# Four graph layers on one core: stored edge matrices loaded sooner into buffers of their own, and edges numbered by ScalarE and TensorE from a transposed adjacency

## The chip, the cores and the metric

The kernel runs on one core of a Trainium2 chip. The metric is the device time of one execution in microseconds, from the first instruction to the last.

## The reference

Eight batches of 2048 nodes with 128 features pass through four layers over one sparse symmetric adjacency (each pair is joined with a chance of about 1/128, and every node with itself). Layers 0 and 2 are multi-head attention with a feed-forward part; layers 1 and 3 are graph attention with additive scores.

```python
def mha(adj, h):                     # layers 0 and 2, 8 heads of 16
    Q, K, V = h @ Wq, h @ Wk, h @ Wv             # split into heads
    scores = einsum('bnhd,bmhd->bhnm', Q, K) / sqrt(16)
    scores = where(adj == 0, -inf, scores)
    x = layer_norm(h + softmax(scores) @ V @ Wo + bo)
    return layer_norm(x + relu(x @ W1 + b1) @ W2 + b2)

def gat(adj, x):                     # layers 1 and 3
    h = x @ W
    e = leaky_relu((h @ a_src)[:, :, None] + (h @ a_dst)[:, None, :], 0.2)
    e = where(adj == 0, -inf, e)
    return layer_norm(softmax(e) @ h + x)

x = gat(adj, mha(adj, gat(adj, mha(adj, x))))
```

## The kernel before

The kernel does not compute dense attention. It turns the adjacency into lists of edges and gathers only the rows of neighbours. (A dense version, `Dense`, stands behind a branch that is taken only where the lists overflow; it is not run here.)

**Units and tiles.** The nodes are cut into 32 units of 64 nodes. A unit holds its edges in nine tiles of 128 slots, handled as `TG` = 5 steps t = 0 to 4, two tiles a step and one in the last. For each unit there is a matrix `hot` (128 x 960): its first 640 columns send a query to the slots of its edges, its last 320 sum slots back to their owners. Layers 1 and 3 rebuild `hot` from a few numbers; layers 0 and 2 load it from DRAM, where it was stored in 8 bits (`self.hots`).

**Lists.** `block_list(adj, i)` works on 128 nodes, so there are 16 blocks, two units each. It loads 128 rows of the integer adjacency (1 MB) into a `kv` buffer, and one VectorE instruction (L1134) turns them into numbers: 0 where there is no edge, and otherwise 2048 minus the column, from the constant `falling`; its accumulator gives `seen[0]`, the sum of the numbers. Sixteen `max` instructions (L1152) take the eight largest of each 128 columns into `cand`, and five rounds of `max` and `match_replace` (L1171, L1173) take the 40 largest of those. L1174 counts them, L1177 sums them into `seen[1]`. `unit_list` then builds each unit's `hot` (ScalarE L1297, L1299, L1301; TensorE L1321; VectorE L1347, L1350, L1390), its gather indices (L1369), and an 8-bit copy `hot8` (ScalarE L1376) that is stored to DRAM (L1380), by POOL's queue for the first 12 units and by SP's afterwards. The 8-bit copies of units 0 to 2 are kept in their buffers until layer 0 uses them.

**Layer 0 and 2 (`attention`).** `opened` calls `fetch` for a unit: a load of x (L1444), a load of the stored matrix into a `hot8` buffer (L1459), and its conversion into a `hot` buffer by ScalarE (L1466). Each step then gathers keys and values (POOL, L1764), spreads queries over slots (TensorE, L1825), multiplies (VectorE, L1837), reduces to scores (VectorE, L1844), takes exponentials (ScalarE, L1854), weighs the values (POOL, L1870; in some steps VectorE), and sums into the unit's accumulator (TensorE, L1922). After step 4, `after_attention` normalizes (it begins with L1981 on VectorE), runs the output product, both norms and the feed-forward part, writes x to DRAM (L1432) and projects it for the next layer (L1626 or L1628, copies L1544 and L1546, stores L1683 or L1686).

**What sets the order.** Every operation is recorded with a cost, a key and the buffers that it takes; `Plan.order` plays them through before anything is issued, giving each engine the ready operation with the lowest key whose buffers are free. The result is a fixed sequence for each engine. An operation that `holds` a cell takes that buffer when it is issued itself. The list of block i has key `10 * i - LEAD` with `LEAD` = 60, and unit u's steps have keys from `5 * u`, so a list is built about 12 units ahead of its use. In `BY_KEY` stand the tags whose buffers are given out strictly in order of keys. An operation with `port=True` does not start while the other of VectorE and POOL runs one. `hot` has three buffers, shared by lists and attention, `hot8` five, `kv` six, and the PSUM tag `m` three banks, used by nearly all small products.

The head, before the first gather, projects all of x into the key and value table (`load`, `project`) and builds the first lists.

Of the kernel before, what the change touches and what calls it, by code (L numbers as in the profile page):

```python
# [48 lines left out]
ADJ = (-1499, -1495, -1487, -1479, -1471)  # L49

SBUF_BUFS = {
    "kv": 6, "hot": 3, "hot8": 5, "x": 4, "q_sb": 2, "rows": 3, "at": 1, "r": 2, "x1": 2, "hidden": 1, "normed": 2,
    "xnew": 2, "trows": 2, "s": 2, "ex": 7, "var": 2, "rstd": 2, "rc": 2, "te": 2, "e": 4, "w": 3,
    "cand": 2, "aux": 3, "aux16": 3, "unit_aux": 2, "some": 2, "rank_e": 2, "pick": 1,
    "gap": 1, "late": 1,
}
BY_KEY = ("kv", "hot", "x", "q_sb", "acc")
PSUM_BUFS = {"q": 1, "acc": 1, "m": 3}

NEG = -57344.0  # L60
# [742 lines left out]
class Sparse:  # L803
# [12 lines left out]

    def __init__(self, ctx, tc, x, xt, xk, adj, w, out):
        self.tc, self.nc, self.w, self.xt_in, self.xk_in, self.out = tc, tc.nc, w, xt, xk, out  # L820
        self.B, self.N, _ = x.shape
        self.NB = self.N // P
        self.NU = self.N // UNIT
        self.HB = self.B // 2

        def pool(name, **kw):
            return ctx.enter_context(tc.tile_pool(name=name, **kw))

        self.nc.scalar.preload_act_table_set("natural_log_exp_and_others")
        self.const = pool("const", bufs=1)  # L830
        self.dram = pool("dram", bufs=1, space=DRAM)
        self.plan = Plan(self.nc)
        self.op, self.cell = self.plan.op, self.plan.cell
        for tag, bufs in SBUF_BUFS.items():
            self.plan.pool(tag, pool(f"sb_{tag}", bufs=bufs), bufs, tag in BY_KEY)
        for tag, bufs in PSUM_BUFS.items():
            self.plan.pool(tag, pool(f"ps_{tag}", bufs=bufs, space=PSUM), bufs)

        self.constants()
        self.weights_at = [Cell() for _ in LAYERS]  # L840
        self.keys_at = Cell()
        self.late = self.tight = False
        self.whole()
        self.gates = {}

        self.gate = self.keys_at
        keys = self.const.tile([P, 2 * P], F32, name="Wkv_0")
        self.fill(0, (keys[:, 0:P], w[0]["Wk"]), (keys[:, P : 2 * P], w[0]["Wv"]), at=self.keys_at)
        self.layers = [{"Wkv": keys}]


        self.tables = [
            self.dram.tile([self.N, self.B * (2 * P if kind is MHA else P + 2)], F32, name=f"table_{n}")
            for n, kind in enumerate(LAYERS)
        ]
        self.table = [Cell() for _ in LAYERS]
        self.rest = [Cell() for _ in LAYERS]

        self.xd = self.dram.tile([self.NU, P, CH], F32, name="xd")
        self.x_at = [Cell() for _ in range(self.NU)]  # L860
        self.hots = self.dram.tile([self.NU, P, HOT], F8, name="hots")
        self.hots_at = [Cell() for _ in range(self.NU)]
        self.kept = {}
        self.ends_at = [None] * self.NU
        self.t = self.const.tile([P, self.NU, P // GROUP * self.HB], F32, name="t")
        self.t_at = [Cell() for _ in range(self.NU)]
        self.idx = self.const.tile([P, self.NU, TILES], I32, name="idx")
        self.idx_at = [Cell() for _ in range(self.NU)]


        self.owner = self.const.tile([P, self.NU, TG, 2], F16, name="owner")
        self.ends = self.const.tile([P, self.NU, 2], F32, name="ends")
        self.late_ends = self.const.tile([P, LATE, 2], F32, name="late_ends")
        self.shift = self.const.tile([P, LATE, 2], F16, name="shift")

        self.empty = self.const.tile([P, self.NU, TILES], F32, name="empty")


        self.seen = self.const.tile([P, 4, self.NB], F32, name="seen")
        self.stats = self.const.tile([P, 6], F32, name="stats")  # L880
        self.eps = self.fixed("eps", EPS)
        self.half = self.fixed("half", 0.5)
        self.rows_n = self.fixed("rows_n", float(self.N))
        self.huge = self.fixed("huge", 1e30)
# [3 lines left out]
    def constants(self):  # L888
# [27 lines left out]
        for pattern, base, step, part in (  # L916
# [12 lines left out]
            channel_multiplier=0,  # L929
            allow_small_or_imprecise_dtypes=True,  # L930
        )

        self.centre = const.tile([P, P], F32, name="centre")
        nc.vector.tensor_scalar(self.centre, self.ident, -1.0 / P, None, ALU.add)
# [182 lines left out]
    def block_list(self, adj, i):  # L1117
# [11 lines left out]
        )  # L1129
        if i < len(ADJ):  # L1130
            self.clear(buf, ADJ[i])
        op(
            {"DVE": 2.4},
            lambda e: e.scalar_tensor_tensor(  # L1134
                buf.tile[:, N : 2 * N],
                buf.tile[:, 0:N].bitcast(I32),
                0.0,
                self.falling,
                ALU.not_equal,
                ALU.mult,  # L1140
                accum_out=self.seen[:, 0, i : i + 1],
            ),
            key,
            writes=[buf],
            port=True,
        )

        cand = cell("cand", [P, 16, 8])

        def parts(e, q):  # L1150
            for c in range(4 * q, 4 * q + 4):
                e.max(out=cand.tile[:, c, :], in_=buf.tile[:, N + c * N // 16 : N + (c + 1) * N // 16])  # L1152

        for q in range(4):
            op({"DVE": 0.9}, lambda e, q=q: parts(e, q), key + 0.1, reads=[buf], writes=[cand])


        late = 2 * i < LATE
        wide = WIDE + 3 * late
# [3 lines left out]
        def largest(e):  # L1163
            c = cand.tile.rearrange("p q c -> p (q c)")
            if late:
                e.tensor_scalar(
                    some.tile[:, 0:8], cand.tile[:, 15, :], 0.0, 0.0, ALU.is_gt, ALU.add, accum_out=aux.tile[:, DEG + 1 :]
                )
            for r in range(DEG // 8):
                top = aux.tile[:, 8 * r : 8 * r + 8]  # L1170
                e.max(out=top, in_=c)  # L1171
                if r < DEG // 8 - 1:
                    e.match_replace(out=c, in_to_replace=top, in_values=c, imm_value=0.0)  # L1173
            e.tensor_scalar(  # L1174
                some.tile, aux.tile[:, 0:DEG], 0.0, 0.0, ALU.is_gt, ALU.add, accum_out=aux.tile[:, DEG : DEG + 1]
            )
            e.tensor_reduce(self.seen[:, 1, i : i + 1], aux.tile[:, 0:DEG], axis=mybir.AxisListType.X, op=ALU.add)  # L1177
            if late:
                deg = aux.tile[:, DEG : DEG + 1]
                e.tensor_tensor(deg, deg, aux.tile[:, DEG + 1 :], ALU.subtract)  # L1180
# [218 lines left out]
    def parts(self, u):  # L1399

        for hf in range(2):
            yield slice(hf * UNIT, (hf + 1) * UNIT), slice(u * UNIT, (u + 1) * UNIT), hf
# [36 lines left out]
    def fetch(self, n, u, key):  # L1439
# [13 lines left out]
            self.op({"ACT": 1.05}, lambda e: e.copy(hot.tile, hot8.tile), key - 15, reads=[hot8], writes=[hot])  # L1453
            return x, hot
        if LAYERS[n] is MHA:
            hot8 = self.cell("hot8", [P, HOT], F8)
            self.op(
                {"SP": 0.45},
                lambda e: e.dma_start(out=hot8.tile, in_=self.hots[u]),  # L1459
                key,  # L1460
                reads=[self.hots_at[u]],
                writes=[hot8],
                holds=[hot],
                dma=P * HOT,
            )
            self.op({"ACT": 1.05}, lambda e: e.copy(hot.tile, hot8.tile), key + 4, reads=[hot8], writes=[hot])  # L1466
            return x, hot
# [782 lines left out]
    def failed(self):  # L2250

        nc = self.nc
        over = self.const.tile([P, 3, self.NB], F32, name="over")
        nc.vector.tensor_tensor(over[:, 0], self.seen[:, 0], self.seen[:, 1], ALU.not_equal)
        for k, most in ((2, GS), (3, TILES * P)):
            nc.vector.tensor_scalar(over[:, k - 1], self.seen[:, k], float(most), None, ALU.is_gt)
        some = self.const.tile([P, 1], F32, name="some_over")
        nc.vector.tensor_reduce(some, over.rearrange("p a b -> p (a b)"), axis=mybir.AxisListType.X, op=ALU.max)
        ps = self.plan.pools["m"].tile([P, CH], F32, name="ps_n", tag="m")
        nc.tensor.matmul(ps[0:1, 0:1], lhsT=some, rhs=self.ones[:, 0:1], start=True, stop=True)  # L2260
        count = self.const.tile([1, 1], I32, name="count")
        nc.vector.tensor_copy(count, ps[0:1, 0:1])
        return count


# [11 lines left out]
        before[i.engine] = i  # L2277


def net(tc, x, xt, xk, adj, w, out):  # L2280

    with ExitStack() as ctx:
        s = Sparse(ctx, tc, x, xt, xk, adj, w, out)
        s.run(adj)
        count = s.failed()
        in_order(tc)
        failed = tc.nc.values_load(count, min_val=0, max_val=P, skip_runtime_bounds_check_because="a count of partitions")
    with tc.If(failed > 0):
        with ExitStack() as ctx:
            Dense(ctx, tc, x, adj, w, out).run()  # L2290
# [36 lines left out]
```

## Time and profile before

| | us |
|---|---|
| median of three runs | 2874.8 (2871.36 to 2889.16) |
| the profiled execution | 2883.92 |
| its span in the trace | 2882.1 |
| PE busy | 2240.7 (78%) |
| VectorE busy | 2235.1 (78%) |
| ScalarE busy | 1463.8 (51%) |
| POOL busy | 2125.6 (74%) |

The span runs from the first to the last instruction of the trace; the rest of the execution's own time lies around it. The first gather starts at 122.6 us, unit 0 of layer 0 ends at 157.0 and unit 31 at 1110.6 (its L1981). Layer 1 follows until about 1590, layer 2 ends its last unit at 2443.0, and layer 3 takes the rest. Lists are built from 9.8 us (first L1134) to 813 us (last L1376), so most of layer 0 runs beside them. The rows of a waits view name the waiting instruction, what it waited for, the sum in us, how many times and the longest. The lines of the chain of work that ended last give a start, a length and what ran or travelled. Rows of groups by form give the instruction with its tiles and shapes, how many, then busy us and mean ns of one, then idle time before them.

### The profile page before, as it was taken

To read this page: it belongs to the slowest core of one execution; us is meant where nothing else is said; L and a number is where in the kernel's file an instruction comes from. 1 tells how busy PE (TensorE), PEld (TensorE's weight loads), DVE (VectorE), ACT (ScalarE), POOL (GpSimd) and SP (SyncE) were. 2 spreads that over 40 slices of the span, in tenths; PEclk is the share of its full clock that TensorE was granted. 3 is DMA by queue.
4 is the path that set the end of the run, shared out by engine and by line. 5 is a ranking of instruction groups with operands and counts; after the bars stand their busy time and mean duration, and the time that the engine had idled before them with its cause. 6 is when DMAs were issued, how large, how long until landed. Compare 5 with 4: busy or idle time off the path is not lost.

```text
span 2882.1 us, 61343 instructions
## 1 busy us (share of the span) xinstructions
PE 2240.7 (78%) x22816; PEld 1371.7 (48%) x22816; DVE 2235.1 (78%) x3662; ACT 1463.8 (51%) x4968; POOL 2125.6 (74%) x1465
## 2 busy tenths in 40 slices
PE   6577767787788887788786788888888888677775
PEld 4334333343344444666665344444444444565664
DVE  8799887888788897555554888989889889576665
ACT  6555545555555553555554244545545445354443
POOL 1287776778888886666664788889888887677774
PEclk8888898999999999889998799999999999888777
DMA  7888777888899998999999799999999898999996
GB/s 289 318 338 341 302 304 262 347 317 314 329 362 363 384 369 320 371 411 405 403 408 379 284 365 371 365 380 385 376 355 395 348 386 303 360 404 407 397 402 273
DMA packets 248066, 1022.63 MB, mean 355 GB/s; under 512 B 39184, under 2 KB 52880, under 8 KB 175856
## 3 DMA queue, kind: packets, MB, share of 16 engines
q0 software_dynamic: 166464, 864.44, 76.3%
q1 hardware_dynamic: 81296, 154.18, 14.3%
q8 instruction: 183, 3.00, 0.4%
q14 instruction: 123, 1.01, 0.1%
HBM read 978.23 MB, written 88.08 MB: 370 GB/s over the span
## 4 chain that ended last, share of the span: by engine, by line
DMA 33%; PE 19%; POOL 15%; DVE 15%; issue 13%; ACT 4%; POOLq 0%; SPq 0%; DVEq 0%; ACTq 0%
DMA kv<-table,idx 25%; POOL kv L1870 8%; POOL kv L1764 7%; DVE kv L1837 6%; DMA hot<-hots 6%; PE qe L1825 4%; PE acc L1922 4%; PE ps_y L1582 3%; DVE s L1844 2%; PE ps_f L1598 2%; DMA table<-trows 1%; PE ps_p L1626 1%; DVE w L2088 1%; PE ps_t L1555 1%; DVE kv L1870 1%
## 5 line engine op out<-in xcount | busy, mean ns | idle before, releaser
L1764 POOL DMA_INDIRECT kv<-table,idx x1152 | 1189.0, 1032 | 550.5 <-issue 292.3
L1870 POOL TENSOR_TENSOR kv<-kv,ex 128x2048 f32<-128x2048 f32 x260 | 922.5, 3565 | 85.4 <-ACT ex L1854 81.7
L1837 DVE TENSOR_TENSOR kv<-qe,kv 128x2048 f32<-128x2048 f32 (+1 forms) x320 | 663.1, 2072 | 206.6 <-DMA kv<-table,idx 106.2
L1844 DVE TENSOR_REDUCE s<-kv 128x128 f32<-128x2048 f32 (+1 forms) x320 | 660.6, 2064 | 15.7 <-ACT normed L1733 0.5
L1825 PE MATMUL qe<-q_sb,hot 32*128 32x512 f32 (+1 forms) x2304 | 398.6, 697 | 167.2 <-DVE kv L1837 164.5
L1922 PE MATMUL acc<-kv,hot 128*32 128x512 f32 (+1 forms) x2304 | 357.9, 639 | 78.9 <-POOL kv L1870 73.3
L2104 PE MATMUL acc_q<-kv,w 128*32 128x129 f32 (+1 forms) x4608 | 197.8, 308 | 106.0 <-DVE w L2088 93.4
L2088 DVE TENSOR_TENSOR w<-hot,e 128x512 f32<-128x512 f32 (+1 forms) x384 | 221.6, 598 | 67.6 <-ACT e L2078 54.2
L1825 PEld LDWEIGHTS qe<-q_sb,hot 32*128 32x128 f32 (+1 forms) x2304 | 106.3, 196 | 330.7 <-DVE kv L1837 276.5
L1854 ACT ACTIVATE ex<-s 128x128 f32<-128x128 f32 (+1 forms) x320 | 94.8, 297 | 295.3 <-DVE s L1844 260.5
L2104 PEld LDWEIGHTS acc_q<-kv,w 128*32 128x32 f32 (+1 forms) x4608 | 157.8, 127 | 139.3 <-DVE w L2088 109.1
L2066 DVE TENSOR_TENSOR e<-te,kv 128x16 f32<-128x16 f32 (+1 forms) x320 | 58.2, 182 | 194.5 <-DMA kv<-table,idx 192.2
L1598 PE MATMUL ps_f<-x,W 128*128 128x512 f32 (+1 forms) x264 | 160.0, 698 | 50.2 <-ACT x L1743 30.0
L1922 PEld LDWEIGHTS acc<-kv,hot 128*32 128x32 f32 (+1 forms) x2304 | 54.8, 113 | 247.2 <-POOL kv L1870 136.1
L2104 PE MATMUL acc<-kv,w 128*32 128x129 f32 (+1 forms) x2304 | 115.1, 299 | 66.1 <-DVE w L2088 57.1
L1582 PE MATMUL ps_y<-W,hidden 128*128 128x128 f32 x1024 | 164.9, 284 | 0.9 <-ACT hidden L2012 0.8
L1544 ACT COPY trows<-ps_p 128x258 f32<-128x258 f32 (+1 forms) x236 | 111.0, 473 | 102.5 <-PE ps_p L1628 36.1
L2078 ACT ACTIVATE e<-e 128x16 f32<-128x16 f32 (+1 forms) x320 | 65.0, 212 | 192.7 <-DVE e L2073 186.0
L2012 ACT ACTIVATE hidden<-ps_f,b 128x512 f32<-128x512 f32 (+1 forms) x128 | 86.6, 678 | 127.4 <-PE ps_f L1598 124.0
L1582 PEld LDWEIGHTS ps_y<-W,hidden 128*128 128x128 f32 x1024 | 142.7, 200 | 4.2 <-issue 2.4
L1700 ACT ACTIVATE junk<-ps_y 128x128 f32<-128x128 f32 x248 | 68.5, 276 | 130.9 <-PE ps_y L1582 120.2
L1555 PE MATMUL ps_t<-ident,normed 128*128 128x128 f32 x638 | 116.4, 303 | 23.5 <-DVE normed L1735 12.1
(220 smaller groups left out, 4092.7 us busy)
## 6 DMA issues: line engine op xcount, KB each, us to landing
x<-xd SPq DMA_DIRECT2D x96, 256.0 KB
xd<-xnew SPq DMA_DIRECT2D x93, 256.0 KB
kv<-table,idx POOLq DMA_INDIRECT x1152
table<-trows SPq DMA_DIRECT2D x128, 130.0 KB
kv<-adj_dram SPq DMA_DIRECT2D x16, 1024.0 KB
table<-trows SPq DMA_DIRECT2D x32, 512.0 KB
table<-trows SPq DMA_DIRECT2D x64, 256.0 KB
kv<-xk_dram SPq DMA_DIRECT2D x8, 1024.0 KB
```

Source lines behind the costliest of these rows:

```text
L1544: e.copy(out, in_)
L1555: e.transpose(ps.tile[:, b * P : (b + 1) * P], flat(x.tile)[:, b * P : (b + 1) * P], self.ident)
L1582: e.matmul(ps.tile[:, cols], lhsT=of, rhs=w, start=first and b == 0 and k == 0, stop=last and b == count - 1 and k == len(terms) - 1, skip ...
L1598: lambda e: e.matmul(ps.tile, lhsT=w, rhs=x.tile, start=True, stop=True),
L1764: e.indirect_dma_start(out=rows(kv.tile, j), out_offset=None, in_=self.tables[n][0:nodes], in_offset=bass.IndirectOffsetOnAxis(ap=self.idx ...
L1825: e.matmul(qe.tile[:, j, hf, :], lhsT=hot.tile[rows, t * P : (t + 1) * P], rhs=q.tile[rows, :], start=True, stop=True,)
L1837: e.tensor_tensor(k, qe.tile[:, 0:tiles].rearrange("p j h c -> p (j h) c"), k, ALU.mult)
L1844: e.tensor_reduce(s.tile[:, 0 : tiles * heads].rearrange("p (q c) -> p q c", q=2 * tiles), k, axis=mybir.AxisListType.X, op=ALU.add,)
L1870: e.tensor_tensor(v, v, w.unsqueeze(3).to_broadcast([P, 2 * tiles, heads // 2, HD]), ALU.mult)
L1922: e.matmul(out[rows, :], lhsT=hot.tile[:, col : col + GROUP * (3 - tiles)], rhs=rhs[:, 2 * j + hf, :], start=(t == 0), stop=(t == TG - 1),)
L2088: e.tensor_tensor(w.tile[:, :, j : j + tiles, :].rearrange("p x j c -> p j x c"), oh[:, j : j + tiles].unsqueeze(2).to_broadcast(shape), e ...
L2104: e.matmul(acc(b)[at : at + GROUP * (3 - tiles), :], lhsT=w.tile[:, hf * hb + b, j : j + 3 - tiles, :].rearrange("p j c -> p (j c)"), rhs= ...
```

## The change

The stored matrix of layers 0 and 2 is loaded into a tag of its own, `stored`, with two buffers in key order; its load has a key 12 lower and no longer holds a `hot` buffer, which is now taken by the conversion. `hot8` has four buffers in place of five.

The adjacency for lists comes transposed within each 128 x 128 block (prepared with the other inputs; the plain one stays for `Dense`). ScalarE takes the sign of the integers into 16-bit values, with `seen[0]` now the count of edges. `falling` is multiplied by the identity once, block by block, so that a product of a transposed block of signs with it puts the numbers into PSUM in the old orientation. The products go four at a time into a bank of `m`, and the maxima read them there. `seen[1]` becomes the count that L1174 gave. The end check compares sums of counts.

```diff
 SBUF_BUFS = {
-    "kv": 6, "hot": 3, "hot8": 5, "x": 4, ...
+    "kv": 6, "hot": 3, "hot8": 4, "stored": 2, "x": 4, ...
-BY_KEY = ("kv", "hot", "x", "q_sb", "acc")
+BY_KEY = ("kv", "hot", "stored", "x", "q_sb", "acc")
...
+        for c in range(self.NB):
+            part = self.falling[:, c * P : (c + 1) * P]
+            nc.vector.tensor_tensor(part, part, self.ident, ALU.mult)
...
+        def edges():
+            return buf.tile[:, N : N + N // 2].bitcast(F16)
+
         op(
-            {"DVE": 2.4},
-            lambda e: e.scalar_tensor_tensor(
-                buf.tile[:, N : 2 * N],
-                buf.tile[:, 0:N].bitcast(I32),
-                0.0,
-                self.falling,
-                ALU.not_equal,
-                ALU.mult,
-                accum_out=self.seen[:, 0, i : i + 1],
+            {"ACT": 1.7},
+            lambda e: e.activation(
+                edges(), buf.tile[:, 0:N].bitcast(I32), AF.Sign, accum_out=self.seen[:, 0, i : i + 1]
             ),
             key,
             writes=[buf],
-            port=True,
         )
 
         cand = cell("cand", [P, 16, 8])
-
-        def parts(e, q):
-            for c in range(4 * q, 4 * q + 4):
-                e.max(out=cand.tile[:, c, :], in_=buf.tile[:, N + c * N // 16 : N + (c + 1) * N // 16])
-
         for q in range(4):
-            op({"DVE": 0.9}, lambda e, q=q: parts(e, q), key + 0.1, reads=[buf], writes=[cand])
-
+            ps = cell("m", [P, CH], name="ps_a")
+
+            def numbered(e, q=q, ps=ps):
+                for c in range(4):
+                    cols = slice((4 * q + c) * P, (4 * q + c + 1) * P)
+                    e.matmul(
+                        ps.tile[:, c * P : (c + 1) * P],
+                        lhsT=edges()[:, cols],
+                        rhs=self.falling[:, cols],
+                        start=True,
+                        stop=True,
+                    )
+
+            op({"PE": 0.4}, numbered, key + 0.1, reads=[buf], writes=[ps])
+
+            def parts(e, q=q, ps=ps):
+                for c in range(4):
+                    e.max(out=cand.tile[:, 4 * q + c, :], in_=ps.tile[:, c * P : (c + 1) * P])
+
+            op({"DVE": 0.95}, parts, key + 0.1, reads=[ps], **{"joins" if q else "writes": [cand]})
...
-            e.tensor_reduce(self.seen[:, 1, i : i + 1], aux.tile[:, 0:DEG], axis=mybir.AxisListType.X, op=ALU.add)
+            e.tensor_copy(self.seen[:, 1, i : i + 1], aux.tile[:, DEG : DEG + 1])
...
         if LAYERS[n] is MHA:
-            hot8 = self.cell("hot8", [P, HOT], F8)
+            hot8 = self.cell("stored", [P, HOT], F8)
             self.op(
                 {"SP": 0.45},
                 lambda e: e.dma_start(out=hot8.tile, in_=self.hots[u]),
-                key,
+                key - 12,
                 reads=[self.hots_at[u]],
                 writes=[hot8],
-                holds=[hot],
                 dma=P * HOT,
             )
...
+    adjt = adj.reshape(blocks, P, blocks, P).transpose(0, 3, 2, 1).reshape(n_nodes, n_nodes)
```

More of the change, by code (lines that the diff above doesn't have):

```diff
@@ L51 @@
 SBUF_BUFS = {
-    "kv": 6, "hot": 3, "hot8": 5, "x": 4, "q_sb": 2, "rows": 3, "at": 1, "r": 2, "x1": 2, "hidden": 1, "normed": 2,
+    "kv": 6, "hot": 3, "hot8": 4, "stored": 2, "x": 4, "q_sb": 2, "rows": 3, "at": 1, "r": 2, "x1": 2, "hidden": 1, "normed": 2,
     "xnew": 2, "trows": 2, "s": 2, "ex": 7, "var": 2, "rstd": 2, "rc": 2, "te": 2, "e": 4, "w": 3,
@@ L803, with __init__ @@
 class Sparse:
-    def __init__(self, ctx, tc, x, xt, xk, adj, w, out):
+    def __init__(self, ctx, tc, x, xt, xk, w, out):
         self.tc, self.nc, self.w, self.xt_in, self.xk_in, self.out = tc, tc.nc, w, xt, xk, out
@@ L2252, in failed @@
         nc = self.nc
-        over = self.const.tile([P, 3, self.NB], F32, name="over")
-        nc.vector.tensor_tensor(over[:, 0], self.seen[:, 0], self.seen[:, 1], ALU.not_equal)
+        over = self.const.tile([P, 2, self.NB], F32, name="over")
         for k, most in ((2, GS), (3, TILES * P)):
-            nc.vector.tensor_scalar(over[:, k - 1], self.seen[:, k], float(most), None, ALU.is_gt)
-        some = self.const.tile([P, 1], F32, name="some_over")
-        nc.vector.tensor_reduce(some, over.rearrange("p a b -> p (a b)"), axis=mybir.AxisListType.X, op=ALU.max)
+            nc.vector.tensor_scalar(over[:, k - 2], self.seen[:, k], float(most), None, ALU.is_gt)
+        some = self.const.tile([P, 2], F32, name="some_over")
+        nc.vector.tensor_reduce(some[:, 0:1], over.rearrange("p a b -> p (a b)"), axis=mybir.AxisListType.X, op=ALU.max)
+        nc.vector.tensor_tensor(self.seen[:, 0], self.seen[:, 0], self.seen[:, 1], ALU.subtract)
+        nc.vector.tensor_reduce(some[:, 1:2], self.seen[:, 0], axis=mybir.AxisListType.X, op=ALU.add)
         ps = self.plan.pools["m"].tile([P, CH], F32, name="ps_n", tag="m")
-        nc.tensor.matmul(ps[0:1, 0:1], lhsT=some, rhs=self.ones[:, 0:1], start=True, stop=True)
+        nc.tensor.matmul(ps[0:1, 0:2], lhsT=self.ones[:, 0:1], rhs=some, start=True, stop=True)
+        both = self.const.tile([1, 2], F32, name="both_over")
+        nc.vector.tensor_scalar(both, ps[0:1, 0:2], 0.0, None, ALU.not_equal)
         count = self.const.tile([1, 1], I32, name="count")
-        nc.vector.tensor_copy(count, ps[0:1, 0:1])
+        nc.vector.tensor_tensor(count, both[:, 0:1], both[:, 1:2], ALU.add)
         return count
@@ L2277, in in_order, with net @@
         before[i.engine] = i
-def net(tc, x, xt, xk, adj, w, out):
+def net(tc, x, xt, xk, adj, adjt, w, out):
     with ExitStack() as ctx:
-        s = Sparse(ctx, tc, x, xt, xk, adj, w, out)
-        s.run(adj)
+        s = Sparse(ctx, tc, x, xt, xk, w, out)
+        s.run(adjt)
         count = s.failed()
@@ L2311 @@
     xk = parts.transpose(2, 4, 1, 3, 0).reshape(n_nodes // UNIT, P, b * UNIT)
-    args = [give("x_dram", x), give("xt_dram", xt), give("xk_dram", xk), give("adj_dram", np.roll(np.asarray(inputs["adj"]), (-FIRST, -FIRST), axis=(0, 1)))]
+    adj = np.roll(np.asarray(inputs["adj"]), (-FIRST, -FIRST), axis=(0, 1))
+    blocks = n_nodes // P
+    adjt = adj.reshape(blocks, P, blocks, P).transpose(0, 3, 2, 1).reshape(n_nodes, n_nodes)
+    args = [
+        give("x_dram", x),
+        give("xt_dram", xt),
+        give("xk_dram", xk),
+        give("adj_dram", adj),
+        give("adjt_dram", adjt),
+    ]
     weights = []
```

## The prediction

> **What bounds the kernel now.** Read first: stages by the windows view. Its rows are the list phase (units 1 to 19 of layer 0, while later units' edge lists are still being built), the rest of layer 0, the middle of layer 2, and the head before the first gather.
>
> ```profile
> core 0: us, PE busy (x) PEld busy (x) DVE busy (x) ACT busy (x) POOL busy (x), PEclk, DMA share, GB/s
> 189.90:791.00 601.10, 453.55 (x3404) 233.56 (x3401) 501.88 (x645) 325.25 (x1058) 466.74 (x255) 0.89 0.83 315
> 852.70:1067.00 214.30, 181.56 (x1461) 93.35 (x1458) 189.37 (x134) 111.20 (x366) 187.16 (x105) 0.98 0.94 373
> 1690.00:2380.00 690.00, 584.53 (x4656) 301.78 (x4656) 602.31 (x419) 350.94 (x1168) 589.07 (x330) 0.97 0.94 372
> 0.00:122.00 122.00, 81.03 (x362) 61.84 (x363) 103.42 (x389) 80.20 (x233) 12.25 (x50) 0.89 0.79 294
> ```
>
> VectorE is the busiest engine in the first three rows. In the trace a unit ends with L1981 on VectorE: 189.9 for unit 1, 791.0 for unit 19, so 601.1/18 = 33.4 us a unit with lists. Units 21 to 29 end at 852.7 and 1058.0: 25.7 us each. A list-phase unit costs VectorE 501.9/18 = 27.9 us, yet fills it only to 0.835, against 189.4/214.3 = 0.884 later. So something besides work holds this phase. The waits view for layer 0 (us in total, times, longest), and one row for layer 2, tell what:
>
> ```profile
> PEld qe L1825 <- DVE kv L1837: 137.5, 91, 11.3
> ACT ex L1854 <- DVE s L1844: 114.3, 70, 13.3
> POOL kv L1764 <- issue: 94.3, 203, 11.4
> ACT hot L1466 <- DMA hot<-hots: 89.2, 21, 11.5
> ...
> ACT hot L1466 <- DMA hot<-hots: 21.7, 8, 7.7
> ```
>
> The last two rows are ScalarE standing at the conversion of a stored matrix that has not landed. ScalarE's queue is in order: behind L1466 stand the exponentials L1854, which POOL's L1870 needs, and the norms. In 189.9 to 791.0 this wait is 76.4 us, 4.2 us of each 33.4 us unit. The chain that ended last goes through these loads again and again (start, length, what):
>
> ```profile
> 416.93 15.83 DMA hot<-hots
> ...
> 452.18 13.65 DMA hot<-hots
> ...
> 555.74 16.44 DMA hot<-hots
> ```
>
> The loop behind it: a list unit frees its hot buffer at L1376, the load is issued (416.98 for unit 10), it lands, and ScalarE has stood 11.5 us at L1466 until 432.8.
>
> The rows of the work that is moved off VectorE, and rows that price its replacements:
>
> ```profile
> L1134 DVE SCALAR_TENSOR_TENSOR kv<-kv,falling 128x2048 f32<-128x2048 int32 x16 | 44.8, 2802 | 4.3 <-DMA kv<-adj_dram 4.3
> L1152 DVE MAX8 cand<-kv 128x8 f32<-128x128 f32 x256 | 52.3, 278 | 0.1
> L1702 DVE BATCH_NORM_STATS2 stats<-r 128x6 f32<-128x128 f32 x9 | 2.6, 294 | 0.3
> L1702 DVE BATCH_NORM_STATS2 stats<-ps_y 128x6 f32<-128x128 f32 x8 | 2.4, 294 | 1.0 <-PE ps_y L1582 0.6 <-ACT junk L1700 0.4
> L1544 ACT COPY trows<-ps_p 128x512 f32<-128x512 f32 x111 | 64.9, 589 | 44.2 <-PE ps_p L1626 35.5 <-PE ps_aux L1261 3.5 <-DMA table<-trows 3.2
> L1544 ACT COPY trows<-ps_p 128x258 f32<-128x258 f32 x125 | 46.1, 369 | 58.3 <-PE ps_p L1628 36.1 <-DVE t L1666 21.9
> ```
>
> and one of the timeline of TensorE (start, length, line, count):
>
> ```profile
> 680.55 0.35 PE L1321 MATMUL ps_l<-unit_aux,hot 128*128 128x86 f16 x5
> ```
>
> **The change part by part.** *Loads of stored matrices.* The same 61 loads of 120 KB go out on the same SP queue, but ask for no hot buffer, and rank 12 keys (about two units) earlier. In the built order, the VectorE work standing between such a load's issue and its conversion was 2 to 14 us in the list phase, against transfers of 8 to 16 us; in the changed order it is 31 to 58 us. For the first two units of layer 2 it is over 300 us, for the third 16, then about 40. SP passes its table and xd stores with them and is mostly idle, waiting for results (L1432 on ScalarE's xnew alone 691 us), so moved issues of about 0.5 us cost nothing; without that idle time they would cost 61 x 0.5 = 30 us spread over the run. The hot buffer is also free from issue to landing, which a list can use.
>
> What is the wait worth? Two ways for the list phase. Taken whole, it is 89.2 us. From load: after the change VectorE needs 27.9 - 1.5 = 26.4 us a unit (the 1.5 is next); at the later phase's 0.884 that is a unit of 29.9 us, 3.5 us less over 18 units = 63 us. The second already contains the friction that replaces a wait, so I take 62, with bounds of 22 (a quarter of the wait) and 112 (whole wait and all of VectorE's relief there). Layer 2: 21.7 us, of which 3.5 + 7.7 = 11.2 stand at the junction of layers 1 and 2, where gathers stop too; I take 14, bounds 5 and 22. What is late next is VectorE itself, then POOL (25.9 us of L1764 and L1870 a unit; at its later 0.873 that is 29.7).
>
> *Numbering.* Out of VectorE go L1134 with its accumulator read (44.8 + 1.3) and the reduction L1177 (3.0): 49.1 us; in comes a one-column copy, 16 x 0.16 (the one-column L1233 takes 0.153): net 46.6, or 1.46 a unit. The 256 maxima stay but read PSUM. The statistics rows above take 294 ns from SBUF and 294 from PSUM, so I take no change; the dearest pair is L2150 from PSUM (218 ns, eight columns) against L2073 from SBUF (171): 47 ns more, 12 us over all, 0.4 a unit. [...]
>
> ScalarE gets 16 Sign passes over 2048 columns. The two copies give (589-369)/254 = 0.87 ns a column, so 589 + 1536 x 0.87 = 1.92 us, plus an accumulator read of 0.19: 2.1 us, 34 us in all, 17 of them in the eight blocks of layer 0. It carries 18.1 us a unit of 33.4, so the work lies beside VectorE's; without that room it would cost 1.05 a unit, 17 us. The price for integer input is not shown on ScalarE; VectorE's 2283 ns median for it equals its 2286 for f32 at L1837. Zero and 17 are the bounds; I take the friction already in the 0.884.
>
> Sign also takes over the wait for adjacency, and ScalarE's queue stands behind it. The trace's records of that transfer show 8.4 to 12.6 us from issue to landing in layer 0. The changed order puts 5 to 14 us of VectorE work, 9 to 20 of ScalarE work, between the two, so 0 to 4 us of wait in some of eight blocks: bounds 0 and 32 us, taken 6, inside that friction too.
>
> TensorE gets 256 products of 128 columns; five of 86 columns take 0.35 us together in that row, so four take about 0.4: 26 us in all, 13 in layer 0, beside a load of 25.2 us in 33.4. Each group borrows one of three "m" banks until its maxima are done (a rival below).
>
> *Head.* 16 products over the numbering constant, 0.225 each by L1313, put 3.6 us on VectorE while the first adjacency travels (it lands at 9.5). VectorE loses about 20 us there and ScalarE gains 17 plus two waits: with hot8 cut from 5 to 4 and three kept, units 4 and 5 wait for the store before them (unit 3's goes out at 65.4 and lands at 71.9), about 5 us each. 80 + 17 + 10 = 107 us of ScalarE under a head of 122, while the table's stores move anyway. I take 0, bounds -10 and +10. The end check adds three small operations, about 0.6 us. Layers 1 and 3 hold none of the edited work.
>
> **Sum**: 62 + 14 + 0 - 0.6, so 75 us less. The profiled execution took 2883.9 us (span 2882.1), 9 above the median of 2874.8: 2809 by its clock, 2800 by the median.
>
> **The rivals.**
> *The wait changes its name (2850 us).* ScalarE's stand at the stored matrix turns into a stand at adjacency and at VectorE; only a third of the 110.9 us comes back, 37, and 12 go to Sign (1.5 us for each of eight blocks): 25 net. For it: the leads for adjacency are near its 8.4 to 12.6 us, and L1854 already waits 114 us for VectorE. Against it: the phase's load of 0.835, which more work-bound phases exceed.
> *All of it was on the path (2741 us).* 110.9 of waits and half of VectorE's 46.6 us: 134. For it: 80.3 us for units 8 and 9 held 22 us of this wait; without it they would have taken 29. Against: units 10 to 12 had 1.7 us of it and still took 30.3 each.
> *PSUM banks (2911 us, slower).* The numbered blocks take 64 more turns of the "m" pool, whose three banks also carry each unit's ps_t, ps_o, ps_f, ps_y. In the built order a group stands up to 5 us of VectorE work ahead of its maxima, and TensorE, in order, stops where a unit's next step finds no bank. With 32 groups in layer 0, 75/32 = 2.4 us of delay per group undoes the gain; 3.5 us makes 112 - 75 = 37 us slower. For it: in the head ps_p waits for trows, a bank's reader, 5.0 + 3.9 us. Against: no such row is among the 25 longest of layer 0, with five such turns a block already.
>
> **How the numbers follow.** Forecast 0.62, on its own 2765 to 2835; name change 0.16; all on the path 0.12; banks 0.10. A measurement of this kernel tells about 1% (29 us) from no change: half of the name change falls within it. So faster 0.82, same 0.08, slower 0.10. The range runs from 2740 to 2865, leaving out the banks and thin edges.
>
> **What would show it.** Right: L1466's wait (its new line) under 15 us in all; units 1 to 19 at about 30 us; VectorE's load there near 0.88; Sign near 2.1 us; maxima still near 280 ns; the first gather within 10 us of 122. Wrong: Sign waiting over 30 us for adjacency; PE waiting for maxima; units still above 32 us, which would say that order or POOL, not the load, set their length.

## The result, and the profile after

The changed kernel takes 2839.2 us (median of six runs, 2833.9 to 2846.9) against 2880.9 for the kernel before on the same chip: a ratio of 0.986, 95% interval 0.983 to 0.988. Run again later beside other kernels it gave 0.987 (0.984 to 0.990). So it is faster by 38 to 42 us, where 75 were forecast. Its profiled execution has a span of 2836.3 us.

The windows view by stage, changed kernel (list phase, rest of layer 0, middle of layer 2, head):

```profile
core 0: us, PE busy (x) PEld busy (x) DVE busy (x) ACT busy (x) POOL busy (x), PEclk, DMA share, GB/s
199.60:768.40 568.80, 449.83 (x3531) 235.78 (x3531) 480.58 (x628) 346.65 (x1086) 462.81 (x254) 0.92 0.88 333
823.30:1032.10 208.80, 183.56 (x1478) 95.43 (x1478) 185.90 (x131) 114.05 (x379) 183.91 (x104) 0.98 0.97 384
1655.70:2314.70 659.00, 562.20 (x4522) 288.55 (x4524) 585.52 (x409) 343.09 (x1134) 572.08 (x322) 0.98 0.96 378
0.00:132.00 132.00, 93.55 (x496) 72.27 (x496) 92.04 (x360) 89.05 (x229) 15.23 (x53) 0.86 0.77 279
```

Units 1 to 19 fall from 601.1 to 568.8 us, 31.6 a unit. VectorE's work there fell by 21 us (1.46 us a unit would be 26: only seven of the sixteen blocks are numbered in this stretch), but it fills the stage only to 480.6/568.8 = 0.845, hardly more than the 0.835 of before and not the 0.88 that the forecast used. Of the 46 us that the span lost, 32 are in this phase, 15 between the end of layer 0 and unit 0 of layer 2 (layer 1 and its junction), 10 in layer 2; the head gave 10 back, since unit 1 ends at 199.6 instead of 189.9; the rest stays within about 3.

The stored matrices, line L1478 of the changed kernel (what its engine waited for before it, in us, times):

```profile
L1478 ACT CAST hot<-stored x61: 974/992/1028, 216.3 to 2315.6; 128x960 f32<-128x960 fp8e5 x61
...
its engine sat idle before it (us, times) until:
  PE acc L1934: 10.5, 18
  DVE w L2100: 1.6, 2
```

No wait for the load is left (it was 110.9 us); what remains is waiting for a `hot` buffer to come free. The waits of layer 0 now read:

```profile
PEld qe L1837 <- DVE kv L1849: 131.9, 88, 4.5
ACT ex L1866 <- DVE s L1856: 114.9, 77, 6.7
...
POOL kv L1776 <- issue: 88.7, 193, 13.8
...
DVE kv L1849 <- DMA kv<-table,idx: 51.0, 36, 5.9
```

In the last row VectorE, the busiest engine, stands for keys and values that have not been gathered yet. Over the whole of layer 0 the kernel before had this row at the same size; between 190 and 760 us, where the lists are built, it grew from 19.3 us (second line) to 36.0 (third, the changed kernel):

```profile
DVE kv L1837 <- DMA kv<-table,idx: 50.6, 29, 10.6
...
DVE kv L1837 <- DMA kv<-table,idx: 19.3, 10, 5.2
...
DVE kv L1849 <- DMA kv<-table,idx: 36.0, 21, 5.9
```

The rows of the moved work:

```profile
L1167 DVE MAX8 cand<-ps_a 128x8 f32<-128x128 f32 x256 | 54.8, 280 | 7.7 <-PE ps_a L1155 6.5 <-PE ps_aux L1274 1.2
...
L1141 ACT ACTIVATE kv<-kv 128x2048 f16<-128x2048 int32 x16 | 30.6, 1913 | 4.1 <-DMA kv<-adjt_dram 4.1
...
L1155 PE MATMUL ps_a<-falling,kv 128*128 128x128 f16 x256 | 25.1, 234 | 15.3 <-ACT kv L1141 5.1 <-DVE cand L1167 3.8 <-ACT owner L1384 2.3
```

Each single price was as forecast: Sign 1.91 us, its wait for adjacency 4.1 us in all, the products 25.1 us in all, a maximum 280 ns. None of these rows says why half of the gain is missing. One stop of its own does show in the trace. The timeline of VectorE, and the load on SP's queue that it waits for (start, length):

```profile
481.31 0.48 DVE L1042 TENSOR_SCALAR W<-W,mean 128x128 f32<-128x128 f32 x2
492.99 0.16 DVE L1043 TENSOR_TENSOR ln_b<-ln_b,b 128x1 f32<-128x1 f32 x1 [11.20 <-DMA b<-L_b_dram]
```

```profile
476.40 0.55 SPq L991 DMA_DIRECT2D b<-L_b_dram  x1
```

Preparing layer 2's weights, VectorE reaches a one-column addition 5 us after its column was asked for, and stands 11.2 us until it lands. TensorE does nothing in that time, ScalarE stops at 484 and POOL at 487; the DMA engines go on, with a share of 0.96. In the kernel before, the same addition ran 14 us after its loads and did not wait.

### The profile page after: what moved, and what is told of

Read it like the earlier page. It is cut to its first block, busy times and chain, and to the rows that moved or that the text cites. A ratio compares the mean times of both kernels' runs of the same rounds, so it can differ in the third digit from the quotient of the medians.

```text
span 2836.3 us, 61976 instructions
## 1 busy us (share of the span) xinstructions
PE 2244.8 (79%) x23072; PEld 1382.0 (49%) x23072; DVE 2214.4 (78%) x3666; ACT 1493.3 (53%) x4982; POOL 2117.6 (75%) x1465
## 4 chain that ended last, share of the span: by engine, by line
DMA 26%; PE 23%; DVE 18%; POOL 16%; issue 12%; ACT 3%; SPq 0%; POOLq 0%; DVEq 0%; ACTq 0%
DMA kv<-table,idx 23%; POOL kv L1882 10%; DVE kv L1849 8%; POOL kv L1776 7%; PE qe L1837 5%; PE acc L1934 5%; DVE s L1856 3%; PE ps_y L1594 2%; PE ps_p L1638 2%; PE acc_q L2116 2%; PE ps_f L1610 1%; PE ps_o L1594 1%; DVE w L2100 1%; PE ps_t L1567 1%; DVE kv L1882 1%
## 5 line engine op out<-in xcount | busy, mean ns | idle before, releaser
L1837 PE MATMUL qe<-q_sb,hot 32*128 32x512 f32 (+1 forms) x2304 | 391.1, 679 | 174.6 <-DVE kv L1849 170.7
L2116 PE MATMUL acc_q<-kv,w 128*32 128x129 f32 (+1 forms) x4608 | 205.7, 313 | 114.5 <-DVE w L2100 104.8
L1556 ACT COPY trows<-ps_p 128x258 f32<-128x258 f32 (+1 forms) x223 | 103.7, 466 | 131.7 <-PE ps_p L1640 76.2
L1610 PE MATMUL ps_f<-x,W 128*128 128x512 f32 (+1 forms) x264 | 148.4, 650 | 17.0 <-ACT x L1755 7.9
L1594 PE MATMUL ps_y<-W,hidden 128*128 128x128 f32 x1024 | 158.2, 276 | 0.0
L1594 PEld LDWEIGHTS ps_y<-W,hidden 128*128 128x128 f32 x1024 | 136.1, 193 | 3.8 <-issue 3.8
L1567 PEld LDWEIGHTS ps_t<-ident,normed 128*128 128x128 f32 x638 | 73.9, 149 | 119.5 <-ACT normed L1745 42.0
```

Source lines behind the costliest of these rows:

```text
L1556: e.copy(out, in_)
L1567: e.transpose(ps.tile[:, b * P : (b + 1) * P], flat(x.tile)[:, b * P : (b + 1) * P], self.ident)
L1594: e.matmul(ps.tile[:, cols], lhsT=of, rhs=w, start=first and b == 0 and k == 0, stop=last and b == count - 1 and k == len(terms) - 1, skip ...
L1610: lambda e: e.matmul(ps.tile, lhsT=w, rhs=x.tile, start=True, stop=True),
L1837: e.matmul(qe.tile[:, j, hf, :], lhsT=hot.tile[rows, t * P : (t + 1) * P], rhs=q.tile[rows, :], start=True, stop=True,)
L2116: e.matmul(acc(b)[at : at + GROUP * (3 - tiles), :], lhsT=w.tile[:, hf * hb + b, j : j + 3 - tiles, :].rearrange("p j c -> p (j c)"), rhs= ...
```

## The experiments

Set A (four kernels on a chip where the kernel before takes about 2877 us) takes the change apart.

**Loads alone** (the kernel before with the new loads):

```diff
-    "hot8": 5,
+    "hot8": 4, "stored": 2,
-BY_KEY = ("kv", "hot", "x", "q_sb", "acc")
+BY_KEY = ("kv", "hot", "stored", "x", "q_sb", "acc")
-            hot8 = self.cell("hot8", [P, HOT], F8)
+            hot8 = self.cell("stored", [P, HOT], F8)
...
-                key,
+                key - 12,
-                holds=[hot],
```

> Only the loads of stored matrices are changed (own buffers, ranked 12 keys earlier, four hot8 buffers); the numbering stays on VectorE. Theory: the list phase was held by ScalarE standing at L1466 (76.4 us of 601), and the units fall to what VectorE's load allows. Here VectorE keeps its 27.9 us a unit, so at the utilisation of 0.845 that the changed kernel showed a unit takes 33.0 us: units 1 to 19 gain only about 7 us, layer 2 gains its 20, the first gather is late by up to 6 (four hot8 buffers): about 2855 to 2865, 0.8% under before. Rival (the wait itself was on the path, the numbering brings nothing): the gain of the changed kernel comes back whole, about 2835, units 1 to 19 near 569 us. Second rival (load and order were independent): half, units near 585.

Measured: 2821.4 us, ratio 0.981 (0.979 to 0.984). Units 1 to 19 took 541 us. My theory (33.0 us a unit, since VectorE keeps its work) fell; the first rival did better than it said, for this kernel is faster than the whole change. VectorE fills its list phase to 495.5/540.7 = 0.916, more than in any row shown of the kernel before:

```profile
197.30:738.00 540.70, 426.24 (x3373) 220.91 (x3377) 495.51 (x648) 324.99 (x1058) 466.15 (x253) 0.93 0.90 347
```

**Numbering alone** (the changed kernel with five `hot8` buffers and the loads as before).

> Only the numbering is moved to ScalarE and TensorE; stored matrices are loaded into hot8 (five buffers) when the hot buffer is free, as before. Theory: ScalarE still stands at the stored matrices in the list phase (70 to 90 us) and its work has grown by 1 us a unit, so VectorE's relief of 1.4 us a unit shows only in part: units 1 to 19 at 590 to 600 us, layer 2 as before, 2870 to 2880, within 0.5% of before. The first gather is late by 5 us or more if ScalarE's Sign is what delays it. Rival (VectorE's relief brings the gain): units 1 to 19 near 570 us, total 2845. Rival (the two parts need each other): no gain here and none in the other.

Measured: 2884.4 us, ratio 1.003 (1.001 to 1.005): no gain, if anything 8 us lost, though VectorE's busy time fell from 2235 to 2210 us. In the profile it was 20 us ahead at unit 19 and 5 at unit 31. ScalarE's stand at the stored matrices was 55.3 us in all against 110.9 before, so half of that wait went with no gain at the end: a row of waits is no price. (Part of it may have been lost again to the buffers held longer, below.)

So the two parts do not add up as forecast. The loads carry all of the gain that was measured, and the numbering costs part of it.

**Without the stop at L1043** (the changed kernel):

```diff
-        op({"DVE": 1.2}, centre, key - 5000, writes=[at], port=True)
+        op({"DVE": 1.2}, centre, key - 5000, reads=[self.t_at[14]] if n else [], writes=[at], port=True)
```

> The changed kernel, with one thing moved: the centring of layer 2's weights and biases (L1043, VectorE) may run only after unit 14 of layer 0, 130 us later, when its small column has long landed. Theory: the stop of 11.2 us on VectorE at 481.9 to 493.0, in which all engines stand, goes; units 1 to 19 take 556 to 560 us instead of 569, the total is 9 to 12 us below the changed kernel (about 2828). Rival (the stop is slack that other waits take over): units 9 to 12 gain it and it is lost again by unit 19, total within 4 us of the changed kernel.

Measured: 2829.9 us, ratio 0.983 (0.980 to 0.986), against 0.986 and 0.987 for the changed kernel: the intervals overlap. In the profile units 1 to 19 took 556.8 us, 12 less; but of the 11 us by which unit 19 ended sooner than in the changed kernel, 3 were left at the start of layer 2 and none at its end (span 2836.7 against 2836.3). The stop is real; whether its 11 us reach the end of the kernel stays open. Nor did the edit move the stop alone: the time for which adjacency buffers are held, counted below, fell with it, from 642 to 531 us.

**Five `hot8` buffers** (the changed kernel with `"hot8": 5, "stored": 2`).

> The changed kernel with five hot8 buffers instead of four (two stored ones kept). Theory: the first gather came 6 us later and unit 2 ended 13 us later than before since units 4 and 5 found no hot8 buffer and ScalarE stood there; with five buffers half of that comes back: first gather at 123 to 126, unit 2 at 225 to 230 instead of 238, total 3 to 8 us below the changed kernel. Rival (the 17 us of Sign on ScalarE in the head set it): first gather within 1.5 us of 128.7, total unchanged within 3 us.

Measured: 2841.9 us, ratio 0.989 (0.986 to 0.991). First gather at 129.0, unit 0 at 168.0: no help. The rival holds for this kernel.

**The suspect.** The adjacency travels into a `kv` buffer, one of six that the gathers need too. Counting from the load's issue on SP to the last read of the buffer, blocks 9 to 15 held theirs 304 us in all before, 257 with the loads alone, 642 in the changed kernel and 683 with the numbering alone: on VectorE numbering and maxima of a block followed each other closely; now its four groups of products stand apart in TensorE's order, the first and the last of a block 18 to 68 us from each other. Set B ran on another chip, where the kernel before takes 3107.3 us, so its times stand beside that number only.

**Numbered sooner** (the changed kernel):

```diff
-            op({"PE": 0.4}, numbered, key + 0.1, reads=[buf], writes=[ps])
+            op({"PE": 0.4}, numbered, key - 20, reads=[buf], writes=[ps])
-            op({"DVE": 0.95}, parts, key + 0.1, reads=[ps], ...)
+            op({"DVE": 0.95}, parts, key - 20, reads=[ps], ...)
```

> The changed kernel, with the products and the maxima of a block ranked 20 keys earlier, so that they follow the Sign pass at once. Why: in the changed kernel a block of layer 0's later eight holds its kv buffer, one of six, for 26 to 108 us from the load's issue to the last product (668 us for the eight); with the numbering on VectorE it was 19 to 70 (327 us, in the run with the loads alone). Gathers of keys and values need these buffers. Theory (holding the buffer is what the numbering costs): holds of 15 to 35 us, units 1 to 19 back to 535 to 545 us, total 2810 to 2825, at or under the run with the loads alone. Rival (the added work on ScalarE and TensorE and its place in their queues costs it): units 1 to 19 stay at 560 to 570, total 2830 to 2840. Rival (PSUM banks): worse than the changed kernel, as four groups now ask for banks at once.

**Held** (the loads alone, plus):

```diff
+        if i > 8:
+            op(
+                {"ACT": 0.2},
+                lambda e: e.copy(self.held, buf.tile[:, N : N + 1]),
+                key,
+                reads=[buf, self.idx_at[2 * i - 1 - i % 2]],
+            )
```

> The kernel with the loads alone (numbering on VectorE), with one thing added: for blocks 9 to 15 a copy of one column on ScalarE that reads the block's kv buffer only after a later unit's list is built, so that the buffer is held 65 to 100 us, as in the changed kernel. No other work is moved. Theory (holding costs it): units 1 to 19 go from 541 to 560 to 570 us, total 2840 to 2850 against 2821. Rival (work and queues): within 5 us of the loads alone.

**Work added** (the loads alone, plus the following, with L1134 reading the signs that ScalarE left in place):

```diff
+        signed = Cell()
+        op({"ACT": 1.7}, lambda e: e.activation(buf.tile[:, 0:N], buf.tile[:, 0:N].bitcast(I32), AF.Sign, ...), key, writes=[buf, signed])
...
+        for q in range(4):
+            ps = cell("m", [P, CH], name="ps_a")
+            def products(e, ps=ps):
+                for c in range(4):
+                    e.matmul(ps.tile[:, c * P : (c + 1) * P], lhsT=self.before, rhs=self.before, start=True, stop=True)
+            op({"PE": 0.4}, products, key + 0.1, reads=[signed], writes=[ps])
```

> The kernel with the loads alone, with the work of the numbering added on the other engines and none taken off VectorE: a Sign pass over 2048 columns on ScalarE, in place ahead of VectorE's L1134, and 256 products of 128 columns in f16 on TensorE into the three m banks behind it, whose results nobody reads. The holds grow only a little. Theory (holding): 3 to 10 us over the loads alone, 2825 to 2832. Rival (the work on ScalarE and TensorE is what costs): 20 us or more, 2842 or over.

**Not sooner** (the loads alone, but with `key` in place of `key - 12`).

> The kernel with the loads alone, but ranked as before (no 12 keys): the stored matrix has buffers of its own and no longer needs the hot buffer. Splits the gain of the loads, 55 us, into buffer and rank. Theory: the load was late since it was issued only when a hot buffer came free, and goes now as soon as one of the two stored buffers is free, whatever its rank; over three quarters of the gain stays, 2820 to 2835. Rival: the rank does it, and without it half is lost, 2850.

Measured in set B ("hold" is the sum for blocks 9 to 15, "units" the time from unit 2 to unit 19):

| | hold, us | units, us | median, us | ratio to before (95%) |
|---|---|---|---|---|
| not sooner | 264 | 516.0 | 3044.8 | 0.981 (0.979 to 0.983) |
| held | 582 | 527.1 | 3065.3 | 0.988 (0.985 to 0.990) |
| work added | 349 | 522.9 | 3058.5 | 0.985 (0.982 to 0.988) |
| numbered sooner | 171 | 523.4 | 3052.7 | 0.984 (0.981 to 0.986) |

"Not sooner" has the whole gain of the loads: 0.981 is what the loads alone gave in set A, on the other chip. The buffers of their own are what counts; a gain from the rank was not seen. The loads alone were not run in set B, so "not sooner" stands for them. "Held" is 20 us slower than that, with no work moved, as the theory wanted. Its profile was taken of the fastest of its six runs (3046.8 to 3074.7 us): it is 11 us behind at unit 19, 8 at unit 31, and not at all at the end (span 3045.1 for both), so where the 20 us of the median arise is not shown. "Work added" lost 14 us, between the two expectations; its holds had grown by 85 us, so work and holding are not told apart by it. "Numbered sooner" could not be judged without the changed kernel beside it.

**Set C** put the main kernels side by side (the kernel before: 2878.1 us).

> The changed kernel once more, beside the three others of this call on one chip, since the two earlier sets ran on chips that differ (3107 us against 2877 for the kernel before). Expected ratio to before 0.984 to 0.988.

> The loads alone once more, on the same chip as the changed kernel. If the numbering costs time, this is 0.4 to 0.9% below the changed kernel, in profile (units 1 to 31) 20 to 30 us; if the gap of the first set came from the chance of single runs, the two are within 0.2%.

> The changed kernel with products and maxima 20 keys sooner, on the same chip. Theory (the held buffer is over half of the cost): half or more of the gap between the changed kernel and the loads alone comes back. Rival (added work and a longer head): it stays within 0.2% of the changed kernel.

> The loads alone with five hot8 buffers instead of four (two stored ones kept). The only thing by which that kernel's head differs from before is four hot8 buffers and the stored ones. Theory: the head's 8 us (unit 0 ends at 165 against 157) come from hot8 and go: unit 0 at 156 to 160, the first gather at 122 to 125, total 3 to 8 us under the loads alone. Rival (the order of the head is another, whatever the buffers): unit 0 stays at 163 to 168 and the total within 0.2%.

| | hold, us | units, us | median, us | ratio to before (95%) |
|---|---|---|---|---|
| changed, again | 635 | 529.8 | 2840.2 | 0.987 (0.984 to 0.990) |
| loads alone, again | 258 | 510.4 | 2820.4 | 0.982 (0.979 to 0.985) |
| numbered sooner, again | 165 | 507.0 | 2820.7 | 0.982 (0.979 to 0.984) |
| loads alone, five `hot8` | 258 | 506.5 | 2817.5 | 0.981 (0.978 to 0.983) |

Every run of "numbered sooner" (2815 to 2824 us) lies below every run of the changed kernel (2828 to 2846). The two do the same work on the same engines; only the rank of products and maxima differs, and with it the time for which the buffer is held and the time at which the lists are done. For block 11, the load's issue and the products of the changed kernel (first and last start behind the durations):

```profile
L1127 SPq DMA_DIRECT2D kv<-adjt_dram x1: 338/338/338, 339.2 to 339.2; - x1
```

```profile
L1155 PE MATMUL ps_a<-falling,kv x16: 216/219/230, 366.3 to 417.3; 128*128 128x128 f16 x16
```

and of the kernel with the numbering sooner:

```profile
L1127 SPq DMA_DIRECT2D kv<-adjt_dram x1: 339/339/339, 338.1 to 338.1; - x1
```

```profile
L1155 PE MATMUL ps_a<-falling,kv x16: 219/219/314, 356.7 to 361.0; 128*128 128x128 f16 x16
```

78 us against 23 for the same 16 products. By the kernel's order it is POOL's gathers that need such a buffer, and VectorE that needs the gathers. The profile names no buffer as what a gather waits for; POOL's idle time before them is put down to "issue". It is longest in the changed kernel, and so is VectorE's wait for gathers. From 190 to 760 us, first POOL and then VectorE, in the changed kernel, the loads alone, and the numbering sooner:

```profile
POOL kv L1776 <- issue: 57.2, 96, 13.6
...
POOL kv L1763 <- issue: 44.2, 109, 4.2
...
POOL kv L1776 <- issue: 43.1, 107, 3.4
```

```profile
DVE kv L1849 <- DMA kv<-table,idx: 40.7, 21, 6.1
```

```profile
DVE kv L1836 <- DMA kv<-table,idx: 26.1, 18, 5.6
```

```profile
DVE kv L1849 <- DMA kv<-table,idx: 20.0, 13, 3.8
```

So the gap of 20 us between the changed kernel and the loads alone comes from the late rank of products and maxima, for an earlier rank gives it all back. That it is the buffer is the likeliest reading, and "held" speaks for it, since it moves no work and ranks no list later; but sooner maxima also finish the lists sooner, which "numbered sooner" does not separate. What neither run shows is a gain from VectorE's relief. Units 1 to 19 of the loads alone, and of the numbering sooner:

```profile
200.20:746.10 545.90, 438.53 (x3370) 226.85 (x3366) 490.97 (x649) 326.14 (x1057) 466.66 (x253) 0.91 0.90 344
```

```profile
209.20:742.00 532.80, 435.77 (x3482) 230.12 (x3482) 471.48 (x603) 337.13 (x1069) 455.76 (x250) 0.94 0.91 350
```

(Unit 1 ended 9 us late in the second and unit 2 did not, so units 2 to 19 are the fair measure: 510.4 and 507.0.) VectorE has 19 us less to do and the phase is 3 us shorter. Either its load does not set the pace at 30 us a unit, or the work added elsewhere takes the relief back; no run here tells which. The DMA engines are a third candidate that no run tests: their share in these two rows is 0.90 and 0.91, against 0.83 in the kernel before.

With the loads alone, five `hot8` buffers help the head a little. POOL's wait for the 8-bit copies, up to 135 us, with four and with five:

```profile
POOL hots L1380 <- ACT hot L1376: 89.6, 8, 23.2
```

```profile
POOL hots L1380 <- ACT hot L1376: 52.9, 6, 16.3
```

The first gather starts at 127.2 instead of 131.4 (129.0 in the profile of set A, also with four), unit 0 ends at 160.3 instead of 167.3 (164.5). By time the two can't be told apart (2817.5 and 2820.4), but this is the version with the lowest median of all that ran, and like the loads alone it beats both the kernel before and the changed one.

## Why the prediction was right or wrong

- **Direction and range.** Faster, as forecast; 2839 is inside 2740 to 2865, but outside the forecast's own 2765 to 2835. About half of the 75 us came. That the wide range held was luck as far as the sum goes: its upper end was there for a rival, and the sum counted a gain for the numbering, which cost time.
- **Wait at the stored matrix, right.** Its row was to fall under 15 us and fell to none for the load. Layer 2 with its junction was put at 14 us, bounds 5 to 22; between the end of unit 31 in layer 0 and the end of layer 2, layer 1 included, the profiles gained 25 in the changed kernel, 17 when it ran again, and 20 with the loads alone.
- **The list phase: this step failed.** I divided VectorE's reduced work by the utilisation of a later stage (26.4/0.884) and said that this "already contains the friction that replaces a wait". It gave 62 us; 32 came in the profile. Two things are wrong in it. The loads alone, with VectorE's work untouched, took 55 to 60 us off units 1 to 19 at a utilisation of 0.90 to 0.92, so 0.884 was no limit, and no run shows the relief as a part of the gain. And the stage kept its lists, so it had a friction of its own which the later stage hasn't got: most likely the buffer of the adjacency. The row that gave 0.884 also has the DMA engines at 0.94, busier than VectorE; what their share would become was not asked. The forecast's 29.9 us a unit was met only where that friction was small (29.8 to 30.0 from unit 2 to 19 in three kernels of set C, 31.2 in the changed one).
- **Numbering: the sign was wrong.** I took 1.46 us a unit of gain inside that quotient. Alone it gave 1.003 (1.001 to 1.005), and on top of the loads it cost 13 to 20 us (by the ratios, by the medians). For Sign I weighed the wait for adjacency, for the products the three banks; I did not ask how long the buffer that they read stays taken. With its readers ranked sooner the numbering cost nothing and gained nothing (2820.7 against 2820.4). In the changed order, the distance from its load to the last product could be read before any run.
- **Single prices, right.** Sign 1.91 + 0.20 us (2.1 forecast), its wait 4.1 us (6), products 0.39 us for four (0.4). The maxima kept 280 ns with a PSUM source against 278 from SBUF.
- **Head: at the edge of its bounds.** Taken as 0, -10 to +10; unit 1 was 10 us late, and the first gather 6. Two causes lie beside each other: with the numbering on VectorE five `hot8` buffers bring unit 0 to 160.3, from 164.5 and 167.3, with the numbering on ScalarE they change nothing (168.0), and the numbering alone, with five, has 165.9.
- **The rivals.** "The wait changes its name" (2850) came nearest in kind: 2839 is 11 us from it, 39 from the forecast. But the new wait is not ScalarE's for adjacency, as it said; it is VectorE's for gathers (19.3 to 36.0 us between 190 and 760). "All of it was on the path" (2741) is 98 us off in the changed kernel, though the loads alone brought back 55 to 60 us of the 76 us of that wait in the list phase. "PSUM banks" is not borne out: VectorE waited 6.5 us in all for products, TensorE 3.8 for maxima. That the products are spread out is the order that the planner built; whether TensorE's turn or a free bank decides it there is not shown.

## What to carry to other kernels

When work moves to another engine, ask not only what it costs there, but how long it now keeps the buffers that it reads: the path through two more queues held a gather buffer some 90 us a block (642/7) instead of some 40, and the kernel lost about a third of the 57 us that the loads alone brought. If buffers must be shared, rank the last reader right behind the first. And the utilisation of one stage does not price another: run each part of a change alone to see which carries the gain.

## What the runs showed of the hardware

- A load of one column (128 packets of 4 bytes), issued at 476.4 us among gathers and five other small loads on its queue, landed at about 493: over 16 us for 512 bytes, about as long as the longest transfer of a stored matrix of 120 KB that the forecast shows (16.44 us). VectorE, which came to it early, stood 11.2 us.
- The same program took 3107 us on one chip and 2877 on others. The difference lies mostly in layers 1 and 3: between the profiles of the loads alone in set C and of "not sooner" they differ by 98 us each, of 228 in all. Layer 1 with the loads alone (set A), and (second fence, other chip) with the rank left as before:

```profile
1150.00:1540.00 390.00, 307.24 (x4674) 239.92 (x4672) 208.98 (x701) 210.80 (x731) 245.74 (x233) 0.90 1.01 398
```

```profile
1150.00:1660.00 510.00, 406.54 (x5310) 298.84 (x5307) 236.03 (x809) 239.49 (x846) 273.12 (x260) 0.88 0.93 334
```

The last numbers are GB/s: 398 against 334 at nearly the same granted clock. Units 1 to 19, which move 347 and 339 GB/s, differ by 2% (540.7 and 552.6 us), and in the middle of layer 2 both kernels move close to 380 (381 and 378). The cause is not shown.
